# The projection of a Mamba scan in two parts and two slots, a front matmul one slot earlier, and a third buffer for the step sizes

## The chip, the cores and the metric

The kernel runs on one core of one Trainium2 chip. The metric is the time of one execution on the device in microseconds (us), as the median of several runs. A difference of about 0.2% (20 us) is what a measurement of this kernel can tell from none. PE is TensorE, PEld its weight loads, DVE VectorE, ACT ScalarE, POOL GpSimd, and SP the engine whose queue issues the DMAs.

## The reference

Four layers run one after the other on an image of 4 x 96 channels x 64 x 64. Layers 0 and 2 are the ones that matter here: two Mamba blocks each, then a fusion with a global branch and a batch normalisation. Layer 1 is a scan of another kind in four directions, layer 3 a convolution block. Cut to its core, one Mamba block is:

```python
def _mamba_block(seq, ln_g, ln_b, in_w, conv_w, conv_b, xproj_w, dt_w, dt_b, A_log, Dp, out_w):
    ...                                                   # h = layer norm of seq
    xs, z = jnp.split(h @ in_w, 2, axis=-1)               # 192 channels each
    ...                                                   # xc = silu(causal convolution of xs, 4 taps)
    dbl = xc @ xproj_w                                    # dt (6), B (16), C (16)
    delta = jax.nn.softplus(dt @ dt_w + dt_b)             # the step sizes
    dA = jnp.exp(delta[..., None] * A)
    dBx = delta[..., None] * Bm[:, :, None, :] * xc[..., None]
    hstates = jax.lax.associative_scan(comb, (dA, dBx), axis=1)[1]
    y = jnp.einsum('blds,bls->bld', hstates, Cm) + Dp * xc
    return (y * jax.nn.silu(z)) @ out_w
```

Each layer adds the block to its input, twice. All numbers are float32.

## The kernel before, in words

`mamba_fusion` takes the images in two pairs. A pair goes through the first block (`sub` 0), then the second (`sub` 1), in 8 chunks of 512 positions. A **step** is one pair, one block and one chunk, so a layer has 32 steps, and both layers 64. Of the two images' 2 x 192 channels, 128 rows at a time form a **block** `j` of three. With 16 states to a channel a block has 2048 recurrences; a **unit** is 256 of them, two tiles of 128 x 512. A step has 24 units, eight to a block.

`Scan.run` writes the order of the work by hand. Its loop index `n` counts units, and in each iteration it emits for several units the stage that is due: the loads of `da` and `du` from DRAM (`load`, five units ahead), the exponentials on ACT (`decay`, `exps`, L111, two ahead), the matmuls that spread `du` over the states into `bs` (`spread`, L343, one ahead), the scan on DVE (`scan`), the product with C on POOL (`after`, L381, one behind), the sums over the states on PE into `py` (`sums`, L400, three behind). In 18 of the 24 units DVE multiplies `bs` (L369) before its two scans (L374); in six the factor comes from DRAM, POOL multiplies it (`product`, L351), there is no L343 and no L369, and ACT writes its exponentials into the buffer of `bs`.

A block is closed four units behind its last one: DVE multiplies `py` by the gate (`close`, L408). `py` has one buffer, so the first sum of the next block waits for L408. When the second and the third block are closed, one image of the pair is complete. Five units behind, `project` emits three matmuls in one go: the residual (L416) and the two halves of the output projection (L418), all into `po`, which has one buffer. Six units behind, ACT copies `po` out (`keep`, L425 in the first block, L574 with a sum over the row in the second); in the second block `spread_out` then squares the copy (L583) and stores it by a DMA (L586), and `reload` fetches the next pair's chunk (L591).

Between all this the next step's front runs: `mamba_front` is a generator whose steps are drawn at a given pace, `PACE`, in the slot of the iteration, `(n + LEAD) % 24`. **Slot** `s` is thus an iteration's place in its step; the unit scanned in it is number `s - 4` of its step. Slots 7, 15 and 23 close the blocks; projections stand in slots 0 and 8. The front's steps 0 to 5 are the layer norm (the matmuls `pc` and `pv`, L190 and L184, with the normalising multiplies L178), 6 to 17 the convolution (`pu`, L205, a step to each tap, four taps to each of three tiles, with the copy L210 into `xz` drawn with the step after a tile's last tap), 18 to 20 the gate (`pz`, L215), 21 `pd` (L228), 22 its copy, and 23 to 28 the step sizes. `pv` uses `po`'s buffer, and so does `w` in the softplus. `xz` has two buffers, one to a step.

The step sizes: for each block a matmul `pt` (L269), four ACT operations, and then on DVE L297 into a tile `delta` and L299; one front step later POOL adds the two (L251) and multiplies (L252), and one later again SP stores both to DRAM (L246: `dd<-delta`, `dg<-du`). `delta` has two buffers, so the third L297 of a step, in slot 21, writes the buffer whose store is issued in the same slot.

What sets the order: at the end of each iteration, every instruction that was emitted is tied behind the last one of its engine, so that each engine runs exactly in the order written. Waits between engines come from the tiles: a write into a buffer waits for its last readers.

Of the kernel before, what the change touches and what calls it, by code (L numbers as in the profile page):

```python
# [18 lines left out]
F32 = mybir.dt.float32  # L19
# [8 lines left out]
P = 128  # L28
T = 512
# [25 lines left out]
ROWS = (((0, 0, 128), (1, 0, 64)), ((1, 64, 128), (2, 0, 128)))  # L55
# [103 lines left out]
def mamba_front(tc, k, X, pools, wt, pair, c, h, made):  # L159
# [84 lines left out]
    for n in range(6):  # L244
# [20 lines left out]
        if n < 3:  # L265
            pt = bank("pt")
            for r0, r1, d0, d1, b in SEGS[n]:
                half = ds(HALFP * b, HALFP)
                nc.tensor.matmul(  # L269
                    pt[r0:r1], lhsT=wt["dt"][half, d0:d1], rhs=dbl[half], start=True, stop=True,  # L270
                )
            kept.append(softplus(nc, k.act, work, psum, pt))
# [3 lines left out]

PACE = (1,) * 6 + (2, 1) * 5 + (1,) * 8
LEAD = 4  # L280


def softplus(nc, act, work, psum, x):

    u = work.tile([P, T], F32, tag="ua", name="ua", bufs=2)
    t = work.tile([P, T], F32, tag="lg", name="lg", bufs=2)
    nc.scalar.activation(u, x, AF.Abs)
    act.exp_ln(u, u, AF.Exp, scale=-1.0)
    act.exp_ln(t, u, AF.Ln, bias=1.0)
    w = psum.tile([P, T], F32, tag="po", name="w", bufs=1)  # L290
    nc.scalar.activation(w, u, AF.Identity, bias=1.0)
    return work.tile([P, T], F32, name="delta", bufs=2), t, u, w, x


def softplus_rest(nc, out, t, u, w, x):
# [6 lines left out]
class Scan:  # L302
# [107 lines left out]
    def project(self, g, b):  # L410

        nc = self.tc.nc
        xz, wt = g["made"]["xz"], g["wt"]
        po = self.po = self.psum.tile([P, T], F32, tag="po", name="po", bufs=1)[:C]
        xs = self.X[:, b, ds(g["c"] * T, T)]
        nc.tensor.matmul(po, lhsT=wt["of_x"], rhs=xs, start=True, stop=False)  # L416
        for n, (j, r0, r1) in enumerate(ROWS[b]):
            nc.tensor.matmul(  # L418
                po, lhsT=wt["out"][r0:r1, j], rhs=xz[r0:r1, j], start=False, stop=(n == 1)
            )  # L420

    def keep(self, g, b):
        xs = self.X[:, b, ds(g["c"] * T, T)]
# [5 lines left out]
    def run(self, steps, wts, front, first):  # L429

        units = [(j, q, p) for j in range(3) for q in range(NQU) for p in range(2)]
        made = [first] + [{} for _ in steps[1:]]
        groups = [
            dict(
                pair=pair, sub=sub, c=c, wt=wts[sub], made=made[n], j=j, q=q, half=p, quarters=(p, p + 2),
                first=(q == 0 and p == 0), last=(q == NQU - 1 and p == 1),
                dma=(q % 2 == 0 and p == 1),
            )
            for n, (pair, sub, c) in enumerate(steps) for j, q, p in units
        ]  # L440
        total, each = len(groups), len(units)
        ahead = iter(())
        traced = self.tc.nc.cur_bb.bb.instructions
        last = {}
        for n in range(-5, total + 10):
            start = len(traced)
            slot = (n + LEAD) % each
            if slot == 0:
                for _ in ahead:
                    pass  # L450
                step = (n + LEAD) // each + 1
                ahead = front(step, made[step]) if 0 <= step < len(steps) else iter(())

            def at(lag):
                return groups[n - lag] if 0 <= n - lag < total else None

            for stage, lag in (
                (self.load, -5), (self.spread, -1), (self.decay, -2), (self.after, 1),
                (self.product, -2), (self.scan, 0),
            ):  # L460
                if g := at(lag):
                    stage(g)
            if (g := at(4)) and g["last"]:
                self.close(g)

            def completed(*stages):

                for lag, what, subs in stages:
                    if (g := at(lag)) and g["last"] and g["j"] and g["sub"] in subs:
                        what(g, g["j"] - 1)  # L470

            completed((6, self.keep, (0, 1)), (7, self.spread_out, (1,)), (8, self.reload, (1,)))
            for _ in range(PACE[slot] if slot < len(PACE) else 0):
                next(ahead, None)
            if g := at(3):
                self.sums(g)
            completed((5, self.project, (0, 1)))

            for ins in traced[start:]:
                if ins.engine not in self.engines:  # L480
                    continue
                if ins.engine in last:
                    self.tc.add_manual_dep(ins, last[ins.engine].name, IN_ORDER, reason="order")
                last[ins.engine] = ins
# [1093 lines left out]
```

## Time and profile before

| | |
|---|---|
| median of 3 runs | 10032.81 us (10032.8 to 10038.04) |
| the profiled execution | 10043.1 us, span 10041.4 us |
| stretch of the first Mamba layer | 0 to 3090 us: PE busy 2573.36, DVE 2682.18, POOL 2472.37, ACT 1827.41 |
| stretch of the second Mamba layer | 6360 to 9460 us: PE busy 2586.69, DVE 2730.21, POOL 2523.79, ACT 1830.90 |
| granted PE clock, whole span | 0.911 |
| DMA engines, busy share in the Mamba layers | 0.73 |

The stretches are read from the busy times by window. A step takes about 96.4 us. No engine is busy all the time, and three of them are above 80%, so the shares alone do not tell which one sets the time at a given place: that is read from the timeline, slot by slot.

### The profile page before, as it was taken

The page shows a single profiled execution, that of the slowest core. Times are in us where ns is not written, and L with a number is a line of the kernel's source. Part 1 is how long each engine was busy: PE and PEld are TensorE (multiplying, and loading weights), DVE is VectorE, ACT ScalarE, POOL GpSimd, SP SyncE. Part 2 cuts the span into 40 slices and gives each one's busy share as a digit, 9 for nine tenths or more (in the row PEclk, how much of TensorE's full clock was granted, in tenths as well). Part 3 has the DMA queues.
Part 4 walks back from the last instruction along what each step waited for, and adds up shares of the span by engine and source line. Part 5 has one row for each costly group of instructions (what it writes and reads, how often), then busy time and mean ns, then how long its engine had stood idle before and what let it go on. Part 6 is the DMA issues. An engine that isn't in the chain of part 4 may idle for free.

```text
span 10041.4 us, 110079 instructions
## 1 busy us (share of the span) xinstructions
PE 8451.2 (84%) x32896; PEld 3485.0 (35%) x32896; DVE 8060.8 (80%) x10870; ACT 5551.0 (55%) x10786; POOL 6873.5 (68%) x4573
## 2 busy tenths in 40 slices
PE   7888888888887888888888888788888888888678
PEld 1112111121212676766766766111211112121122
DVE  6888888888886666766666767688888888898887
ACT  5565665656654545555555544556565565665345
POOL 6888888888875555555555555588887888888511
PEclk8889898999987999999999999799999999998789
DMA  7777777777775222322322321777777776777653
GB/s 183 191 199 189 202 200 202 197 188 199 199 192 154 76 66 81 87 67 82 87 66 77 86 66 55 181 193 201 188 203 194 203 198 188 198 197 197 167 120 84
DMA packets 813857, 1531.94 MB, mean 153 GB/s; under 512 B 126893, under 2 KB 132425, under 8 KB 809802
## 3 DMA queue, kind: packets, MB, share of 16 engines
q1 hardware_dynamic: 810186, 1519.79, 56.7%
q8 instruction: 260, 4.26, 0.2%
q10 hardware_dynamic: 3072, 5.11, 0.1%
q14 instruction: 339, 2.78, 0.1%
HBM read 1229.28 MB, written 148.50 MB: 137 GB/s over the span
## 4 chain that ended last, share of the span: by engine, by line
PE 50%; DVE 28%; ACT 7%; issue 6%; DMA 4%; POOL 3%; SPq 1%; DVEq 0%; POOLq 0%; ACTq 0%
DVE hs L374 12%; PE py L400 9%; PE bs L343 7%; PE pu L205 6%; PE front L976 6%; DVE bs L369 5%; PE front L987 3%; DMA dd<-delta 3%; PE po L418 3%; PE y L1070 2%; DVE seg L1025 2%; PE pz L215 2%; DVE yz L1092 2%; PE pc L190 2%; DVE acc L1370 2%
## 5 line engine op out<-in xcount | busy, mean ns | idle before, releaser
L381 POOL TENSOR_TENSOR hc<-hs,bc 128x1024 f32<-128x1024 f32 x1536 | 3617.1, 2357 | 1045.2 <-DVE hs L374 993.8
L374 DVE TENSOR_TENSOR_SCAN hs<-da,carry,bs 128x512 f32<-128x512 f32 x2016 | 2470.7, 1267 | 120.0 <-DVE bs L369 1.4
L343 PE MATMUL bs<-du,seldu 64*128 64x512 f32 x4608 | 1463.5, 690 | 700.0 <-DVE hs L374 699.2
L400 PE MATMUL py<-hc,selsum 128*32 128x512 f32 x6144 | 1687.7, 657 | 234.6 <-DVE xz L408 221.3
L369 DVE TENSOR_TENSOR bs<-bs,bc 128x1024 f32<-128x1024 f32 x1152 | 1399.5, 1215 | 407.7 <-PE bs L343 407.0
L111 ACT ACTIVATE da<-da,w_a 128x512 f32<-128x512 f32 x2304 | 1518.0, 710 | 0.0
L343 PEld LDWEIGHTS bs<-du,seldu 64*128 64x128 f32 x4608 | 397.3, 199 | 1720.4 <-DVE hs L374 1185.7
L351 POOL TENSOR_TENSOR du<-du,bc 128x1024 f32<-128x1024 f32 x384 | 905.6, 2358 | 49.2 <-DMA du<-dg 49.2
L1025 DVE TENSOR_SCALAR seg<-dr,dac 128x128 f32<-128x128 f32 x1536 | 638.9, 450 | 278.6 <-PE y L1070 275.8
L111 ACT ACTIVATE bs<-da,w_a 128x512 f32<-128x512 f32 x768 | 528.8, 689 | 585.3 <-DVE hs L374 572.2
L1041 POOL TENSOR_TENSOR seg<-seg,cb 128x384 f32<-128x384 f32 x512 | 515.7, 1009 | 475.0 <-DVE cb L1040 410.8
L205 PE MATMUL pu<-h,w_conv 96*128 96x512 f32 (+3 forms) x2048 | 822.3, 638 | 0.5 <-POOL h L179 0.5
L374 DVE TENSOR_TENSOR_SCAN hs<-bs,carry,du 128x512 f32<-128x512 f32 x672 | 818.8, 1259 | 0.0
L976 PE MATMUL front<-pk,sconv 128*128 128x512 f32 x1536 | 754.1, 608 | 25.5 <-ACT z L964 22.2
L400 PEld LDWEIGHTS py<-hc,selsum 128*32 128x32 f32 x6144 | 224.0, 112 | 1527.2 <-issue 1146.7
L1080 POOL TENSOR_TENSOR y<-y,xs 128x192 f32<-128x192 f32 x496 | 295.9, 597 | 604.2 <-DVE y L1079 582.8
L1093 ACT ACTIVATE y<-yz 128x192 f32<-128x192 f32 x512 | 186.1, 363 | 900.9 <-DVE yz L1092 900.2
L384 ACT COPY carry<-hs 128x2 f32<-128x2 f32 x1344 | 247.4, 184 | 737.2 <-DVE hs L374 735.4
L1045 POOL TENSOR_TENSOR xs<-pre,coef 128x576 f32<-128x576 f32 x512 | 598.5, 1174 | 55.9 <-ACT pre L116 25.3
L987 PE MATMUL front<-sconv,pk 128*128 128x192 f32 x3072 | 572.1, 329 | 57.5 <-DVE pre L992 52.2
L987 PEld LDWEIGHTS front<-sconv,pk 128*128 128x128 f32 x3072 | 496.3, 190 | 90.1 <-DVE pre L992 79.0
L1070 PEld LDWEIGHTS y<-xs,seg 128*128 128x128 f32 x3072 | 437.3, 204 | 142.5 <-issue 79.5
(227 smaller groups left out, 13771.6 us busy)
## 6 DMA issues: line engine op xcount, KB each, us to landing
da<-dd SPq DMA_DIRECT2D x3072, 256.0 KB
du<-dg SPq DMA_DIRECT2D x768, 256.0 KB
dr<-rows SPq DMA_DIRECT2D x256, 384.0 KB
bc<-rows SPq DMA_DIRECT2D x256, 256.0 KB
dd<-delta SPq DMA_DIRECT2D x192, 256.0 KB
dg<-du SPq DMA_DIRECT2D x192, 256.0 KB
pk<-xn SPq DMA_DIRECT2D x128, 384.0 KB
pk<-xn SPq DMA_DIRECT2D x128, 256.0 KB
```

Source lines behind the costliest of these rows:

```text
L111: self.last = self.scalar.activation(out, in_, func, **kw)
L205: nc.tensor.matmul(pu[r0:r1], lhsT=wt["conv"][:kk, tap, d0:d1], rhs=h[:kk, b, ds(tap, T)], start=(tap == 0), stop=(tap == 3),)
L343: nc.tensor.matmul(g["bs"][:, i], lhsT=self.sel["du"][rows, g["half"], g["q"]], rhs=g["made"]["du"][rows, g["j"]], start=True, stop=True,)
L351: self.tc.nc.gpsimd.tensor_tensor(g["du"], g["du"], self.b_or_c(g, 0), ALU.mult)
L369: nc.vector.tensor_tensor(dbx, dbx, self.b_or_c(g, 0), ALU.mult)
L374: nc.vector.tensor_tensor_scan(hs[:, i], da[:, i], dbx[:, i], init, ALU.mult, ALU.add)
L381: nc.gpsimd.tensor_tensor(g["hc"], hs, self.b_or_c(g, 1), ALU.mult)
L400: nc.tensor.matmul(py[rows], lhsT=self.sel["sum"][:, g["q"]], rhs=g["hc"][:, i], start=(g["q"] == 0), stop=(g["q"] == NQU - 1),)
L976: nc.tensor.matmul(p, lhsT=self.conv[:, i, DI + q * DST : DI + (q + 1) * DST], rhs=pk[:, i, ds(c * T, T)], start=(i == 0), stop=(i == 2),)
L987: nc.tensor.matmul(p, lhsT=pk[:, i, ds(c * Q, Q)], rhs=self.conv[:, i, :DI], start=(i == 0), stop=(i == 2),)
L1025: nc.vector.tensor_scalar(seg[:, h], g["pair"]["dr"][:, c % 2 * NH + h], made["dac"][:, n0 + h : n0 + h + 1], 0.0, ALU.subtract, ALU.min,)
L1070: nc.tensor.matmul(py[:, ch], lhsT=seg[:, h], rhs=xs[:, 0, ch], start=True, stop=True)
```

## The change

Three things are changed, and nothing is computed differently. `project` emits the residual and the first half of the projection; a new stage `project_rest` emits the second half one slot later, in slots 1 and 9, and the keeping copy, the square with its store, and the reload follow one slot later each. In `PACE`, the two front steps of slot 8 and the one of slot 7 change places, so that step 9, the last tap of the first convolution tile, is drawn in slot 7 instead of 8; the slots of all others stay. And `delta` has three buffers instead of two. The loop runs one iteration more.

```diff
-PACE = (1,) * 6 + (2, 1) * 5 + (1,) * 8
+PACE = (1,) * 6 + (2, 2, 1, 1) + (2, 1) * 3 + (1,) * 8
...
-    return work.tile([P, T], F32, name="delta", bufs=2), t, u, w, x
+    return work.tile([P, T], F32, name="delta", bufs=3), t, u, w, x
...
         nc.tensor.matmul(po, lhsT=wt["of_x"], rhs=xs, start=True, stop=False)
-        for n, (j, r0, r1) in enumerate(ROWS[b]):
-            nc.tensor.matmul(
-                po, lhsT=wt["out"][r0:r1, j], rhs=xz[r0:r1, j], start=False, stop=(n == 1)
-            )
+        j, r0, r1 = ROWS[b][0]
+        nc.tensor.matmul(
+            po, lhsT=wt["out"][r0:r1, j], rhs=xz[r0:r1, j], start=False, stop=False
+        )
+
+    def project_rest(self, g, b):
+        j, r0, r1 = ROWS[b][1]
+        self.tc.nc.tensor.matmul(
+            self.po, lhsT=g["wt"]["out"][r0:r1, j], rhs=g["made"]["xz"][r0:r1, j], start=False,
+            stop=True,
+        )
...
-        for n in range(-5, total + 10):
+        for n in range(-5, total + 11):
...
-            completed((6, self.keep, (0, 1)), (7, self.spread_out, (1,)), (8, self.reload, (1,)))
+            completed((7, self.keep, (0, 1)), (8, self.spread_out, (1,)), (9, self.reload, (1,)))
...
-            completed((5, self.project, (0, 1)))
+            completed((5, self.project, (0, 1)), (6, self.project_rest, (0, 1)))
```

## The prediction

> **What bounds the kernel now.** I read the table of busy times by stretch first, then the waits, then the timeline of two steps. The stretches 0 to 3090 us and 6360 to 9460 us are the two Mamba layers, 64 steps of 24 slots; the change touches nothing else. One step, from the second closing multiply to the next one, and the 37 us in it that follow the last closing multiply, look like this (columns: stretch, length, then busy us and count of PE, weight loads, DVE, ACT, POOL, then the granted clock, the DMA share, GB/s):
>
> ```profile
> 1038.26:1134.70 96.44, 79.28 (x250) 18.55 (x250) 85.63 (x79) 59.31 (x115) 79.10 (x39) 0.92 0.74 202
> 1038.26:1041.50 3.24, 2.51 (x5) 0.61 (x6) 3.11 (x5) 3.20 (x6) 3.24 (x2) 0.50 0.42 128
> 1070.37:1107.77 37.40, 37.40 (x127) 9.08 (x128) 34.05 (x30) 25.41 (x49) 29.80 (x14) 1.00 0.73 196
> ```
>
> VectorE has the most work (85.63 of 96.44 us), but in the last row PE has no idle time at all: there PE sets the pace and DVE fits itself in. So the step has two regimes. What DVE waits for, in the list of waits (us, times, longest), with the two rows of the others that matter:
>
> ```profile
> DVE bs L369 <- PE bs L343: 407.0, 146, 12.7
> ACT xz L210 <- PE po L418: 338.0, 60, 8.4
> PE py L400 <- DVE xz L408: 221.3, 118, 3.2
> DVE delta L297 <- DMA dd<-delta: 171.6, 61, 4.1
> ```
>
> I put the waits of the trace to their slots by counting the scans off 24 to a step. DVE idles per step 3.0 us before its multiply L369 of slot 2, 2.85 us before that of slot 10, 2.8 us before the third L297 in slot 21, and in no other slot over 0.6 us. The places in the timeline (start, length, engine, line, idle before and its releaser in brackets), first slots 7 to 10 and one later pair, then slots 21, 23 and 2:
>
> ```profile
> 1068.48 1.12 PE L205 MATMUL pu<-h,w_conv 96*128 96x512 f32 x2
> 1070.37 1.05 PE L400 MATMUL py<-hc,selsum 128*32 128x512 f32 x4 [0.77 <-DVE xz L408]
> 1071.35 2.14 PE L205 MATMUL pu<-h,w_conv 97*128 97x512 f32 x6
> 1075.43 2.12 PE L418 MATMUL po<-xz,w_out 64*96 64x512 f32 x4
> 1077.48 1.13 PE L343 MATMUL bs<-du,seldu 64*128 64x512 f32 x4
> 1077.59 0.59 ACT L210 COPY xz<-pu 128x512 f32<-128x512 f32 x1 [5.16 <-PE po L418]
> 1078.66 1.23 DVE L369 TENSOR_TENSOR bs<-bs,bc 128x1024 f32<-128x1024 f32 x1 [2.37 <-PE bs L343]
> 1094.40 1.13 PE L343 MATMUL bs<-du,seldu 64*128 64x512 f32 x4
> 1095.81 1.21 DVE L369 TENSOR_TENSOR bs<-bs,bc 128x1024 f32<-128x1024 f32 x1
> ...
> 1029.47 0.69 DVE L297 SCALAR_TENSOR_TENSOR delta<-pt,lg 128x512 f32<-128x512 f32 x1 [3.41 <-DMA dd<-delta]
> 1038.99 1.92 PE L400 MATMUL py<-hc,selsum 128*32 128x512 f32 x4 [3.15 <-DVE xz L408]
> 1047.50 1.23 DVE L369 TENSOR_TENSOR bs<-bs,bc 128x1024 f32<-128x1024 f32 x1 [2.59 <-PE bs L343]
> ```
>
> The reader is to see one pattern twice: DVE closes a block (L408), PE has stood idle for it (0.77 and 3.15 us), then PE works through sums, front matmuls and three projection matmuls before it reaches the `bs` that DVE needs next.
>
> [...]61 waits of DVE on the stores of `delta`, a pool of two. [...]here the store issued at 1023.63 released DVE at 1029.35, 5.7 us later, and I use the trace. [...]the second row of the first fence shows 0.50 after idle time.
>
> **The change, part by part.** PE prices at full clock from the timeline: front matmul 1.03 us (a pair of rows), projection matmul 1.03, `py` 0.98, `bs` 1.06. No instruction is added or removed; 64 steps move three matmuls, and the keeping copies with the stores and reloads behind them go one slot later.
>
> (a) Slots 7 to 10. The front matmul of tap 3 goes from slot 8 to slot 7, ahead of the `py` that waits for the close. It fills the 0.77 us of idle time, so `py` starts 0.26 late and everything behind it is 1.03 - 0.26 = 0.77 earlier. The second projection matmul goes behind slot 9's `bs`, so that `bs` is 1.03 + 0.77 = 1.8 us earlier and the wait of 2.37 falls to some 0.6. But the matmul is not gone: from slot 10's `bs` on, PE is only 0.77 ahead of before. DVE may use what reserve it had: in slot 15 `bs` ended at 1095.46 and DVE took it at 1095.81, 0.3 us net of the 0.05 that a handover takes. So DVE gains 0.77 + 0.3, about 1.05, and the rest comes back as small waits in slots 11 to 18. Over the 62 steps that have all these slots, min(idle before `py`, 1.03) plus the smallest reserve in slots 11 to 19, and never more than the wait itself, averages 0.88. 62 x 0.88 = **55 us**.
>
> (b) Slot 21. With a third `delta`, no buffer is used twice in a step, so L297 waits for no store of its own step; stores of the step before landed long ago. Next is the multiply of slot 22: its `bs` had been ready 5.9 us on average (5.9 - 2.8 = 3.1 left); `t`, `u` and `w` come from ACT before the stall (1024.3). POOL is without a gap there until 1030.5 and then catches up part of the time; its next reader on DVE's path is the product for slot 1, done 3.1 us ahead of its scan, 1.3 then. The later loads from DRAM are issued five slots ahead, and no wait of ACT on them stands in the list. So the whole wait goes: 171.6 us, and 6.5 us (3 times) where the store was late enough that POOL's read was the releaser: **178 us**.
>
> (c) Slots 0 to 2. The second projection matmul goes behind slot 1's `bs`: DVE's multiply of slot 2 starts 1.03 earlier. The next `bs` is not earlier, because PE has the same work before it; its reserve before slot 3 averaged 0.7 net. min(1.03, reserves of slots 3 and 4) averages 0.64. 62 x 0.64 = **40 us**.
>
> (d) Added waits. Slot 2's `pv` writes the single `po` buffer, now kept in slot 2 instead of 1: PE's sums and `bs` stand behind it. ACT needs after the square: two exponentials (1.33), the carry (0.18) and the copy (0.68 + 0.19), about 2.4 us; PE has sums, the second half and a `bs` first, 3.07 us. Hence 0, bound 0 to 1.0 per step. L210 of slot 8 overwrites the `xz` buffer that the projection reads, so it now waits for the half in slot 9: release at about 1079.8 instead of 1077.5. Behind it on ACT stand the exponentials of slot 11, which were done 4.3 us before their scan; 2.2 later release and 1.4 earlier scan leave 0.7. Hence 0, bound 0 to 2 in the steps with half clock. The variance square moves from slot 2 to 3, behind the mean; it no longer waits for `pv` (32.1 us in 28 waits), and ACT idled 0.94 before the second root. Hence 0, bound +-0.5. SP issues the same stores and reloads one slot later, behind loads for five slots ahead. POOL's order stays. One iteration more at each layer's end: under 1 us.
>
> (e) PE's clock: the half clock sits in slots 20 to 23, 0 and 5. Less idle time may spare some of it; `py` and `pc` after the second close took 1.92 + 1.85 instead of 0.98 + 1.03. Up to 1.8 us per step, 110 us, either way. I take 0, since PE still idles over 6 us in slots 21 to 23.
>
> Sum 55 + 178 + 40 = 273 us. The profiled execution took 10043.1 us (span 10041.4), so 9770 in its terms; the median of the runs is 10.3 lower: **9760**.
>
> **Rivals.** *Only the buffer pays*: the second halves return at the next `bs`, `pv` and L210 eat the rest: 10033 - 178 = 9855. For it: PE without idle time in slots 7 to 18; against: the 0.77 us of idle time that are filled. *All three waits go*: 62 x (3.0 + 2.85) + 178 = 541, 9490; between it and mine lies the clock gain, about 9650. Against: PE's 37.40 of 37.40. *Slower*: L210 holds ACT in slot 8 until the exponentials of slot 11 are late in every step. It decides when the copy's idle time passes 5.2 + 4.3 (reserve) + 4.4 (gains), some 14 us; then about +0.7 us per step, 10078. It needs half clock through slots 7 to 9, where half clock begins in 10 of 62 steps; the longest such wait is 8.4. *The change does not do what it says*: another reader still holds `delta`; then 10033 - 95 = 9938.
>
> **How the numbers follow.** Sum as worked out (9700 to 9815): 0.56. Buffer alone, or a and c alone: 0.20. Clock gain or more: 0.16. Slower: 0.05. No change: 0.03. A measurement of this kernel tells 0.2%, 20 us, from no change. The range 9650 to 9870 takes in the clock's 110 us below and the buffer alone with 15 us above. Faster 0.92, same 0.03, slower 0.05.
>
> **What would show it.** The wait on `dd<-delta` is gone. DVE's wait for `bs` falls from 407 to about 310 us, no longer 128 large ones but many small ones in slots 11 to 18. PE's wait for L408 falls by about 54 us (slot 7). L210's wait grows to about 7.4 us each. A step takes about 92.1 us with DVE and PE busy as long as now. Wrong, if DVE waits for ACT in slot 11, if PE waits at `pv`, or if another wait stands in slots 21 to 23.

## The result, and the profile after

The changed kernel takes 9751.71 us (median of 4 runs, 9745.13 to 9757.5) against 10035.42 us before: a ratio of 0.9715, with a 95% interval from 0.9698 to 0.9732. The forecast was 9760. The profiled execution has a span of 9746.5 us, 294.9 less than before.

The list of waits of the changed kernel (engine and line that waited, who ended it; us in total, times, longest us), in the rows that answer to those of before:

```profile
ACT xz L210 <- PE po L424: 428.7, 60, 8.2
DVE bs L369 <- PE bs L343: 233.1, 174, 12.6
PE py L400 <- DVE xz L408: 180.6, 91, 3.2
PE py L400 <- POOL hc L381: 80.9, 32, 3.2
```

The row with `dd<-delta` is gone. DVE's wait for `bs` has fallen from 407.0 to 233.1 us, in more and smaller pieces (174 for 146). PE's wait for L408 seems to have fallen from 221.3 to 180.6, but most of the last row belongs to it: there a product of POOL happened to end at the same moment as the close, and all of slot 23's first sums start 0.15 us after the end of L408, as they did before. With all its causes, PE's idle time before L400 went from 234.6 to 261.5 us. So PE waits longer for the closes than before, by some 27 us.

One step from second close to second close, and the 8 us behind the second close (columns: stretch, length, busy us and count of PE, weight loads, DVE, ACT, POOL, then the granted clock, DMA share, GB/s):

```profile
988.21:1079.92 91.71, 78.30 (x250) 18.57 (x250) 85.95 (x78) 59.03 (x115) 78.88 (x39) 0.95 0.78 212
1079.90:1087.90 8.00, 7.83 (x16) 1.66 (x18) 5.96 (x6) 4.79 (x11) 8.00 (x5) 0.63 1.06 256
```

The step is 4.7 us shorter and DVE has the same work in it (85.95 for 85.63 us). Behind the second close PE is at 0.63 of its clock, less than the 0.78 over the same stretch of the kernel before:

```profile
1038.90:1046.90 8.00, 7.91 (x20) 2.01 (x20) 5.88 (x5) 4.99 (x11) 7.01 (x4) 0.78 0.80 197
```

The timeline of slots 7 to 11 of the changed kernel, and of slots 23 and 2 (start, length, engine, line, idle before and its releaser):

```profile
1016.68 1.99 PE L205 MATMUL pu<-h,w_conv 96*128 96x512 f32 x4
1020.00 1.05 PE L400 MATMUL py<-hc,selsum 128*32 128x512 f32 x4 [1.33 <-DVE xz L408]
1022.98 1.10 PE L416 MATMUL po<-X,fus 96*96 96x512 f32 x2
1024.55 1.41 PE L343 MATMUL bs<-du,seldu 64*128 64x512 f32 x3
1026.00 1.23 DVE L369 TENSOR_TENSOR bs<-bs,bc 128x1024 f32<-128x1024 f32 x1
1027.88 1.10 PE L424 MATMUL po<-xz,w_out 128*96 128x512 f32 x2
1029.02 0.59 ACT L210 COPY xz<-pu 128x512 f32<-128x512 f32 x1 [6.96 <-PE po L424]
...
1080.07 1.92 PE L400 MATMUL py<-hc,selsum 128*32 128x512 f32 x4 [2.28 <-POOL hc L381]
1088.80 1.23 DVE L369 TENSOR_TENSOR bs<-bs,bc 128x1024 f32<-128x1024 f32 x1 [2.81 <-PE bs L343]
```

Taps 2 and 3 now stand together ahead of the sum (1.99 us of `pu`), and PE still idles 1.33 us there, more than the 0.77 of before. DVE's multiply of slot 10 waits for nothing. That of slot 2 still waits 2.81 us in this step.

DVE's idle time by slot, averaged over the 62 steps whose slots lie in one loop, counted from the traces like the numbers of the prediction (us per step):

| slots | before | changed kernel | gain | predicted |
|---|---|---|---|---|
| 2 to 4 | 3.5 | 3.1 | 0.4 | 0.64 |
| 10 to 18 | 3.8 | 1.8 | 2.0 | 0.88 |
| 21 | 2.8 | 0.1 | 2.7 | 2.9 |
| all 24 | 11.2 | 6.1 | 5.1 | 4.4 |

5.1 us by 62 steps is 316 us; DVE's instructions together took 20 us more than before (8080.8 for 8060.8), and some 296 are left, about the difference of the spans.

### The profile page after: what moved, and what is told of

It is laid out like the page before. It is cut to its first block, busy times and chain, and to the rows that moved or that the text cites. A ratio compares the mean times of both kernels' runs of the same rounds, so it can differ in the third digit from the quotient of the medians.

```text
span 9746.5 us, 109952 instructions
## 1 busy us (share of the span) xinstructions
PE 8319.4 (85%) x32896; PEld 3486.3 (36%) x32896; DVE 8080.8 (83%) x10870; ACT 5536.2 (57%) x10786; POOL 6860.0 (70%) x4573
## 5 line engine op out<-in xcount | busy, mean ns | idle before, releaser
L400 PE MATMUL py<-hc,selsum 128*32 128x512 f32 x6144 | 1670.7, 651 | 261.5 <-DVE xz L408 180.6
L369 DVE TENSOR_TENSOR bs<-bs,bc 128x1024 f32<-128x1024 f32 x1152 | 1406.3, 1221 | 254.1 <-PE bs L343 233.1
L205 PE MATMUL pu<-h,w_conv 96*128 96x512 f32 (+3 forms) x2048 | 796.4, 624 | 1.4 <-POOL h L179 1.4
L400 PEld LDWEIGHTS py<-hc,selsum 128*32 128x32 f32 x6144 | 222.4, 111 | 1504.8 <-issue 924.6
```

What stands on the lines that cost most here:

```text
L205: nc.tensor.matmul(pu[r0:r1], lhsT=wt["conv"][:kk, tap, d0:d1], rhs=h[:kk, b, ds(tap, T)], start=(tap == 0), stop=(tap == 3),)
L369: nc.vector.tensor_tensor(dbx, dbx, self.b_or_c(g, 0), ALU.mult)
L400: nc.tensor.matmul(py[rows], lhsT=self.sel["sum"][:, g["q"]], rhs=g["hc"][:, i], start=(g["q"] == 0), stop=(g["q"] == NQU - 1),)
```

## The experiments

Each experiment ran beside the kernel before on the same chip; the ratios are to that.

| kernel | us | ratio, 95% interval |
|---|---|---|
| third buffer alone | 9875.21 | 0.9823 (0.9804 to 0.9841) |
| PACE alone | 9994.24 | 0.9938 (0.9919 to 0.9958) |
| split alone | 10151.32 | 1.0101 (1.0081 to 1.0120) |
| PACE and split | 9943.93 | 0.9894 (0.9871 to 0.9917) |
| split and a filler in slot 7 | 9968.09 | 0.9930 (0.9915 to 0.9944) |
| before and fillers in slot 4 | 10201.36 | 1.0163 (1.0141 to 1.0186) |
| changed, residual earlier | 9616.43 | 0.9577 (0.9563 to 0.9591) |
| changed, fillers in slots 22 and 23 | 9606.79 | 0.9571 (0.9556 to 0.9585) |
| both of these | 9566.31 | 0.9529 (0.9515 to 0.9544) |
| residual, fillers in slot 22 alone | 9577.36 | 0.9541 (0.9525 to 0.9557) |

### The third buffer alone

```diff
-    return work.tile([P, T], F32, name="delta", bufs=2), t, u, w, x
+    return work.tile([P, T], F32, name="delta", bufs=3), t, u, w, x
```

> Before with the third buffer of delta alone. The prediction's step (b) in isolation: the wait of L297 on dd<-delta (171.6 us) goes, nothing takes its place, 10035 - 178 = about 9857. Rival 1 (POOL or the loads take the stall over): less than half of it, above 9945. Rival 2 (the earlier slots 21 to 23 also change PE's half clock after the second close): the wait of L369 in slot 2 moves from 3.0 us by more than 0.3 us either way, and the time by 20 us or more. The half clock in slot 5 should stay, since nothing before it on PE changes.

It took 179 us off (10054.63 to 9875.21; the prediction's step said 178). In slot 21 DVE's idle time went from 2.8 to 0.1 us, and no other slot took it over: slot 2's wait went from 3.09 to 3.22, slot 10's from 2.85 to 2.62. Both rivals fall; the half clock of slot 5 stayed (0.58).

### PACE alone, the split alone, and both

```diff
-PACE = (1,) * 6 + (2, 1) * 5 + (1,) * 8
+PACE = (1,) * 6 + (2, 2, 1, 1) + (2, 1) * 3 + (1,) * 8
```

> Before with the new PACE alone: tap 3 in slot 7, the projection in one go. Theory: it fills the 0.87 us of PE's idle time before slot 7's first sum; slot 10's wait falls from 2.85 to about 2.1 us; 62 x 0.74 = 46 us, about 9990. If the gain in slots 10 to 16 (2.0 us a step in the changed kernel, against 0.88 predicted) comes from the PACE alone: 9910. If it needs the split: 9990 or more. Slot 5 keeps its half clock.

60 us less. Slot 10's wait fell by 1.4 us, to 1.47, not by 0.74: the theory had only the filled idle time. The clock of slot 8 went from 0.92 to 0.99, and that of slot 5, which was to stay, from 0.64 to 0.74.

The split alone is the changed kernel with the lines of PACE and of `delta` put back:

> Before with project_rest alone. Theory of the prediction: slot 2 gains 0.64 us a step; slot 10's wait falls by 1.03 but comes back in slots 11 to 18 except for the reserve of 0.2; 50 us together, about 9985. Theory of the clock: the split in slots 0 to 2 lets DVE reach slot 4 earlier, [...]the half clock of slot 5 goes, and PE is there earlier in slot 7; then slot 10's wait falls by more than 1.03, and the time is about 9930.

It made the kernel slower, by 97 us. Neither theory had that. The half clock of slot 5 did go (0.64 to 0.90), as the theory of the clock said, and slots 2 and 3 gained what they gain in the changed kernel; but slot 10's wait grew to 3.7 us. Two steps of this one profile show why. The first sum of slot 7 with the multiply of slot 10, and the busy times of 8 us behind the close, first in a step where PE idles 0.77 us, then in one where it idles 2.19:

```profile
1078.92 1.05 PE L400 MATMUL py<-hc,selsum 128*32 128x512 f32 x4 [0.77 <-DVE xz L408]
1079.90 2.14 PE L205 MATMUL pu<-h,w_conv 97*128 97x512 f32 x6
1085.97 1.23 DVE L369 TENSOR_TENSOR bs<-bs,bc 128x1024 f32<-128x1024 f32 x1 [1.13 <-PE bs L343]
...
1174.35 1.61 PE L400 MATMUL py<-hc,selsum 128*32 128x512 f32 x4 [2.19 <-DVE xz L408]
1175.90 3.98 PE L205 MATMUL pu<-h,w_conv 97*128 97x512 f32 x6
1184.65 1.23 DVE L369 TENSOR_TENSOR bs<-bs,bc 128x1024 f32<-128x1024 f32 x1 [4.37 <-PE bs L343]
```

```profile
1078.80:1086.80 8.00, 7.88 (x26) 1.93 (x26) 6.74 (x6) 2.15 (x5) 6.99 (x4) 1.00 0.75 208
1174.20:1182.20 8.00, 7.85 (x16) 1.41 (x16) 5.94 (x6) 2.18 (x5) 5.55 (x4) 0.57 0.84 202
```

In the first step the split does what it was thought to do: slot 10's wait is 1.13 instead of 2.37. In the second, the same six matmul rows take 3.98 us instead of 2.14, at 0.57 of the clock, and the wait is 4.37. The half clock came with the longer idle time ahead of the sum; whether it is the cause of the loss, a filler tests below. In this kernel slot 8 ran below 0.75 of the clock in 50 of 62 steps; in the kernel before in 10; in the changed kernel in 2.

> The changed kernel with two buffers of delta again: PACE and split together. Sum of the prediction's (a) and (c): 95 us, about 9940. By what the changed kernel's slots show (2.0 in slots 10 to 16 and 0.4 in slots 2 to 4): 148 us, about 9887. If the parts add up, this gain is that of PACE alone plus that of the split alone; if it is more, filling the idle time in slot 7 and taking a matmul off the way to slot 9's bs need one another.

111 us less: between the two numbers, nearer to the smaller one. The parts don't add up: PACE alone gains 60 and the split alone loses 97, together they gain 111, so 148 us lie in their meeting. The third buffer does add up: 111 + 179 = 290, and the changed kernel gained 284.

### A filler in slot 7

That the clock is the cause, and not the order of the matmuls or the held copy L210, was put to the test by keeping PE busy there without moving any work. Into the split alone:

```diff
+            if slot == 7 and 0 <= n < total:
+                idle = self.psum.tile([P, T], F32, tag="po", name="idle", bufs=1)
+                self.tc.nc.tensor.matmul(
+                    idle, lhsT=self.k.ident, rhs=self.sel["du"][:, 0].rearrange("p q n -> p (q n)"),
+                    start=True, stop=True,
+                )
             if g := at(3):
                 self.sums(g)
```

> The split alone (10151 us, 97 above before) with one matmul of 128 x 512 added in slot 7, ahead of the first sum that waits for the close; its result is not used. It moves no work away from slot 8, it only keeps PE busy in the idle time. Theory of the clock: in the split alone PE reaches slot 7 earlier, idles 1.9 us there and is put on half clock in slots 8 and 9 (0.60 and 0.78), and that is why slot 10's wait grew from 2.85 to 3.7 us. With the filler the clock there is 0.95 or more, slot 10's wait falls to about 1.9 us, and the time to 10151 - 62 x 1.8 = about 10040, in spite of 62 added matmuls. Rival (the second half behind bs, or ACT's copy L210 held until slot 9, is what costs): the wait and the time stay, 10151 or more.

One useless matmul a step turns a loss of 1.0% into a gain of 0.7%. From the timeline, the filler and what follows:

```profile
1052.66 1.02 PE L484 MATMUL idle<-seldu,ident 128*128 128x512 f32 x2
1055.01 1.05 PE L400 MATMUL py<-hc,selsum 128*32 128x512 f32 x4 [1.33 <-DVE xz L408]
1056.00 2.14 PE L205 MATMUL pu<-h,w_conv 97*128 97x512 f32 x6
1062.07 1.23 DVE L369 TENSOR_TENSOR bs<-bs,bc 128x1024 f32<-128x1024 f32 x1 [1.12 <-PE bs L343]
```

Idle time of 1.33 us did not lower the clock here: slot 8 was below 0.75 in none of the 62 steps. Slot 10's wait averaged 1.22 us, less than the 1.9 expected, and the time is 72 us below the 10040 expected. So the tap that PACE moves does two things in slot 7: it takes 1.03 us off the way behind the close, and it keeps the clock. Against the split alone the filler is worth 1.7% (0.9930 / 1.0101) and the tap 2.0% (0.9894 / 1.0101), so most of what the tap gives there is the clock.

### Fillers in slot 4 of the kernel before

```diff
+        if n == 4:
+            idle = psum.tile([P, T], F32, tag="po", name="idle", bufs=1)[:C]
+            for _ in range(2):
+                nc.tensor.matmul(
+                    idle, lhsT=k.center, rhs=X[:, 0, ds(c * T, T)], start=True, stop=True
+                )
```

> Before with two matmuls of 96 x 512 added in slot 4, into the free po buffer, results not used: PE's idle time ahead of slot 5's bs (3.09 us) falls to about 1. Theory: the half clock of slot 5 (0.64) goes to 0.95 or more, PE does slots 5 to 7 faster and reaches the sum of slot 7 about 0.7 us earlier; the work behind the close is the same, so DVE gains nothing by it, and where the longer idle time in slot 7 (0.9 to 1.6 us) puts PE on half clock in slots 8 and 9, slot 10's wait grows: the time is 10035 to 10150. Rival: the half clock of slot 5 costs DVE time of itself; then its removal gains 0.5 us a step or more, 10000 or less.

The theory had the sign and too little of the size: 156 us slower. Slot 5 went to 0.98 of the clock, PE came earlier to slot 7 and waited longer there, and the clock fell behind it instead, in slot 8 in all of the 62 steps (mean 0.51):

```profile
1085.78 1.84 PE L406 MATMUL py<-hc,selsum 128*32 128x512 f32 x4 [2.20 <-DVE xz L414]
1095.72 1.23 DVE L375 TENSOR_TENSOR bs<-bs,bc 128x1024 f32<-128x1024 f32 x1 [4.01 <-PE bs L349]
```

(Lines 400, 408, 369 and 343 stand six lines further down in this kernel.) Making PE faster where nothing waits for it made the kernel slower.

### The residual one slot earlier, and fillers ahead of the second close

The residual matmul needs no closed block. A stage `residual` emits it ahead of the first sum:

```diff
+    def residual(self, g, b):
...
+        self.tc.nc.tensor.matmul(po, lhsT=g["wt"]["of_x"], rhs=xs, start=True, stop=False)
...
-        nc.tensor.matmul(po, lhsT=wt["of_x"], rhs=xs, start=True, stop=False)
...
+            completed((4, self.residual, (0, 1)))
             if g := at(3):
                 self.sums(g)
```

> The changed kernel with the residual matmul (L416), which needs no closed block, one slot earlier: in slots 23 and 7, ahead of the first sum, into po, which is free there. The same mechanism once more: what stands ahead of the wait for the close costs nothing while PE idles there (2.8 us in slot 23, 1.2 in slot 7), and is 1.03 us less on the way to the next bs. Theory: slot 2's wait falls from 2.6 to about 1.6 or less, the small waits of slots 10 to 15 (0.87 us in all) go; 62 x 1.9 = 118 us below the changed kernel, about 9635. Rival: PE's slots 10 to 18 and 2 to 4 are now bound by DVE and gain nothing, only slot 2's wait moves on to slot 3: 9715 or more.

Against the changed kernel, each ratio with its own run of the kernel before: 0.9577 / 0.9715 = 0.986, 1.4% less; the medians, from different runs, are 135 us apart. Slot 2's wait fell from 2.6 to 1.1 us on average, those of slots 10 to 15 from 0.87 to 0.31. The rival falls. Slot 2's wait fell by more than the 1.03 us of the matmul, and the clock of slot 23 rose from 0.62 to 0.81: the residual shortened the way and also spared some half clock, and this run does not tell the two apart.

Into the changed kernel instead, with `n` 4 and 5 of the front's last loop in slots 22 and 23:

```diff
+        if n in (4, 5):
+            idle = bank("idle")
+            for _ in range(2):
+                nc.tensor.matmul(idle, lhsT=k.ident, rhs=dbl, start=True, stop=True)
```

> The changed kernel with two matmuls of 128 x 512 added in slot 22 and two in slot 23, results not used, where PE idles 2.2 us ahead of bs and 2.8 us ahead of the first sum. Theory of the clock: PE is at half clock when the second block is closed (0.62 in slot 23, 0.50 in slot 0), and the sums and pc after it take 1.92 + 1.85 instead of 0.98 + 1.03 us. With the filler the clock in slots 23 to 1 is 0.9 or more, slot 2's wait falls from 2.6 to about 0.9 us: up to 62 x 1.7 = 105 us below the changed kernel, about 9650. Rival: at half clock the added matmuls take twice their time, hold back slot 23's bs and cost DVE in slot 0: the changed kernel's time or more.

Two more matmuls in each of two slots of every step, none of them used, take 1.5% off (0.9571 / 0.9715 = 0.985), 145 us between the medians. Busy times of the 8 us behind the second close, and slot 23's filler with the first sum behind it and the multiply of slot 2 (lines 373, 404 and 412 are here what 369, 400 and 408 are in the changed kernel):

```profile
1055.60:1063.60 8.00, 7.80 (x24) 1.82 (x24) 7.63 (x8) 5.46 (x13) 8.00 (x5) 1.00 1.04 259
```

```profile
1052.50 1.98 PE L276 MATMUL idle<-dbl,ident 128*128 128x512 f32 x4
1055.80 1.05 PE L404 MATMUL py<-hc,selsum 128*32 128x512 f32 x4 [1.31 <-POOL hc L385]
1061.86 1.23 DVE L373 TENSOR_TENSOR bs<-bs,bc 128x1024 f32<-128x1024 f32 x1
```

The clock is 1.00 where it was 0.63, the first sum takes 1.05 us instead of the 1.92 shown for the changed kernel, and the wait of slot 2 is down from 2.6 to 0.16 us on average. So most of that wait was half clock.

Both together, and the residual with fillers in slot 22 alone:

> The changed kernel with the residual one slot earlier and the two added matmuls in each of slots 22 and 23. Theory: what is left of the residual version's wait in slot 2 (1.1 us) is half clock after the close (0.81 in slot 23, 0.56 in slot 0); with the clock kept it goes, and PE's way to slot 2's bs is 1.03 shorter besides; DVE's idle time falls from 4.0 to about 2.9 us a step, 9616 - 62 x 1.1 = about 9550. Rival: residual and fillers together are more than the idle time of slot 23 (2.8 us) holds, so the first sum comes after the close by up to 1 us and the gain is 0 to 20 us.

> As the residual version, with two added matmuls in slot 22 alone, results not used. Theory: the residual fills part of slot 23's idle time itself, so that two matmuls in slot 22 may keep the clock: if the clock in slots 23 and 0 is 0.9 or more, the time is that of the version with fillers in both slots, about 9550; if the clock falls again ahead of the close, it lies between 9550 and 9616.

9566 and 9577: their intervals overlap. The first, 4.7% below the kernel before, beats every other version beyond its interval; the interval of the second just touches that of the fillers in slots 22 and 23. With fillers in slot 22 alone the clock was 0.97 in slot 23 and 0.81 in slot 0, so the time lies between 9550 and 9616, as was expected for that case. Neither version reaches 9550: DVE still idles 3.4 us a step. Of this, 2.6 us lie outside slots 2, 10 and 21; the kernel before already had 2.3 there.

## Why the prediction was right, and where it was not

**The time** (9760 for 9751.7) came out closer than the sum deserves, by luck. In the profiles step (a) gave some 70 us more than predicted, step (c) 17 us and slot 21 some 10 us less, and DVE's own instructions took 20 us more, for which the sum had no term.

- **Step (b), the buffer**: right. 178 us predicted, 179 measured with the buffer alone, and nothing was late next, as worked out from the reserves of slots 22 and 23.
- **Step (a), slots 7 to 10**: mis-sized, 0.88 us a step for 2.0. What was right: the matmul that goes behind `bs` does come back as small waits in slots 11, 12 and 15 (0.1 to 0.3 us each), and DVE uses up PE's reserve there (0.21 us in slot 15 before, 0.01 after). What failed is the limit of 0.87 us for what can be hidden ahead of the close. It was read from a PE that came late to slot 7 after half clock in slot 5. Without that half clock it is there sooner, as the fillers in slot 4 show (its idle time ahead of slot 7's first sum went from 0.87 to 2.20 us), and it hides all of the tap.
- **Step (c), slots 0 to 2**: mis-sized, 0.64 us a step for 0.36. `bs` was to come 1.03 us earlier; the mean wait fell by only 0.5. PE's clock in slot 1 fell from 0.92 to 0.85, so the work ahead of it took longer. That it did so was seen; why it did was not tested.
- **Step (e), the clock**: the step that failed. It was taken as zero, because PE still idles over 6 us in slots 21 to 23. But it gained in slots 5 to 9 (slot 5 from 0.64 to 0.91, slot 8 from 0.92 to 0.98) and lost in slot 1. Nor is it a term of its own that may be set to zero: it decides what (a) is worth, since the split of (a) and (c) without the tap costs 97 us.
- **Step (d), the added waits**: right. L210 waits 428.7 / 60 = 7.1 us each (7.4 predicted), and DVE waits for ACT in slot 11 in none of the 62 steps; at `pv` PE's matmuls wait for the kept copy nowhere, only the weight load does, 60 times and by at most 0.8 us (before, it waited for the carry 82 times, also by at most 0.8 us).
- **Signs**: the `dd<-delta` row is gone, as said; a step takes 91.8 us (92.1 said); the wait for `bs` is 233 us (310 said). That PE's wait for L408 would fall by 54 us was wrong: with the part that stands under POOL's name it grew by some 27.
- **The rivals**: "only the buffer pays" is refuted by PACE and split together (111 us). "All three waits go" failed at slot 2, where 2.6 of 3.1 us stayed. The slower rival had its sign in the split alone, but not its mechanism: there too L210's wait is longer, and the filler in slot 7, which leaves the copy behind the same matmul, takes the loss away. The half clock behind the close was named in it only as a condition.

## What to carry to other kernels

Where two engines wait for one another in turn, put work that doesn't need the other's result ahead of the wait, not behind it; as far as it fits into the idle time it cost nothing here, and it comes off the way to the next result. Before making PE faster or earlier at some place, look where it will then stand idle and what its clock does behind that: an edit that only moves idle time can lose more than it gains (the fillers in slot 4 cost 156 us), and a useless matmul in the right place was worth nearly as much here as a useful one moved (1.7 and 2.0% in slot 7). Moving work past one waiting point gains only the reserve of the points behind it, so read those before counting the wait itself.

## What the runs showed of the hardware that was not expected

- A matmul of 128 x 512 whose result nobody reads, one a step, took 1.7% off the split alone (some 170 us of 10151), and four a step took 1.5% off the changed kernel (some 145 us of 9752).
- Idle times of PE ahead of the first sum of slot 7, in 62 steps of each of the twelve traces: up to 1.62 us, all 608 were followed by full clock in slot 8; at 2.00 us, nine of ten by about half of it; from 2.1 us on, all 126 (0.50 to 0.57 in ten steps of the kernel before, 0.50 in two of the changed one). In the split alone the six matmul rows behind the sum took 3.98 us where 8 us there had 0.57 of the clock, and 2.14 us where they had 1.00.
- The length of the idle time alone does not decide. Ahead of slot 5's `bs` PE idled 2.57 us on average both in the changed kernel and in the one with fillers in slots 22 and 23; slot 5 ran below 0.75 of the clock in 11 of 62 steps of the first and in 58 of the second.
- In the traces of the kernel before and of the changed one the recorded clock is 0.5 or 1.0 throughout (474 and 358 records). The clock given here for a slot is the mean from the slot's first scan to that of the next.
- What sets the clock of slot 5 besides the length of the idle time was not shown.
